# VectorE's order in an attention loop: transposes of projection inputs moved behind the next maxima, two small operations moved to GpSimd, statistics and residual additions moved later

## The chip, the core and the metric

The kernel runs on one core of a Trainium2 chip. The metric is the device time of one execution in microseconds (us); comparisons use the median of several runs. The engines are TensorE (PE; PEld is its weight load), VectorE (DVE), ScalarE (ACT), GpSimd (POOL) and SyncE (SP, which here only issues DMAs).

## The reference

x and ctx have shape [4, 1024, 512], all in fp32.

```python
def reference(x, ctx, Wq, bq, Wk, bk, Wv, bv, Wo, bo, clip_x, clip_down, w_gate, w_up, w_down):
    x = x + xattn(layernorm(x), ctx, ...)       # 16 heads of 32
    x = x + ffn(layernorm(x), ...)              # inner width 1408
    return x
# xattn: q = xn@Wq+bq; k, v = ctx@Wk+bk, ctx@Wv+bv; softmax(q k^T / sqrt(32), masked) @ v; @Wo+bo
# mask: rows 0..767 ("image") attend within their own block of 256; rows 768..1023 ("text")
#       attend to all image columns and causally to text columns
# ffn:  quant(x) = clip(round(x/s), -128, 127)*s, s = sigmoid(clip)*max|x|/127, over the whole tensor
#       weights quantised likewise by row; h = quant(silu(xq@Wg.T) * (xq@Wu.T)); h @ Wd.T
```

## The kernel before, in words

**Units and steps.** The attention is cut into 112 units. A unit is one of the four groups of four heads, for one block of 256 query rows of one batch element; a text block has four parts per group, an image block one. So a batch has 12 image units and 16 text units, and the last batch takes one image block, then text, then two image blocks. The loop `for n in range(len(units) + V_LAG)` makes one step per unit. In step n it issues, in this order:

1. `maxima(units[n])`: the scores s on PE (L449 for image, L460 for text) into PSUM, and their negated row maxima nmh on DVE (L453; L471 with the mask's addition L470). After a unit's last part, `minus_maxima` splits the maxima into two bf16 terms (L481 for text, a cast L488, a subtraction L489), and `shifts` transposes them to nmt (L496) and sends four small DMAs from SP to nmT (L501).
2. One item of the `background` deque: the layer norm of a chunk of 256 rows of x in three items (statistics on DVE L368 and L369, `deviation` on ACT and POOL L373 to L382, `apply` on ACT with the write to xn_d), or a weight's scale (L689 to L691 on DVE) and quantisation (POOL L695).
3. `large(n)`: one part of a projection on PE (pp_q, pp_kv, pv, and po for outputs, all at L229 in a helper). The bank that they write is freed by ACT's copies, or by the addition xr on DVE (L636).
4. Weights of unit n-5: the scores again, transposed (t), with the shift put in by a matmul of nmT (L534) and the products (L539), then exp on ACT (L544, L549); POOL sums the results into sp (L523).
5. Values of unit n-6 (av, L583 and L602), whose quotient (reciprocal L617 on DVE, product oT L618 on POOL) follows in the next step.
6. At the end of the step, `small_step`: a DVE transpose (L270) turns a loaded, spread projection input into qT or kvT, which the next projection reads. It runs only if `can_small(n)`: its load must have been sent in an earlier step. Then `prepare_next(n)` sends the load of the following one (L147, a single buffer), and a `weight_unit` may be queued.

From step 84 (`LATE`) on, projections are made in halves. After the loop come the second layer norm's scales, the FFN (pg and pu at L1219, silu L1227, h L1262, its maximum L1264) and the down stage (pd L1371).

**Who sets the order.** PE, DVE, ACT and POOL run in the order in which the program issues their instructions (`manual_schedule`), so an instruction that waits holds all that follow it on its engine. SP's DMAs are ordered by the scheduler. Scores and transposed scores share three PSUM buffers: t of unit n-5 can go on only when the maxima of unit n have been read.

**The down stage.** For each block of 512 tokens four tiles are multiplied. For each tile DVE quantises a group of the next block's h (L1345, with ACT's cast L1346), scales the product (sd, L1379) and adds it to the residual (L1380). After the block, POOL's queue gets the reload of a spilled h block (L1388) and then the block's output (L1390).

Of the kernel before, what the change touches and what calls it, by code (L numbers as in the profile page):

```python
# [14 lines left out]
ALU = mybir.AluOpType  # L15
# [9 lines left out]
NIC = FF // P  # L25
# [17 lines left out]
def kernel(ctx: ExitStack, tc: tile.TileContext, x, kv, Wq, bq, Wk, bk, Wv, bv, Wo, bo, clip_x, clip_down, w_gate, w_up, w_down, out):  # L43
    nc = tc.nc
# [78 lines left out]
    with ExitStack() as actx:  # L123
# [230 lines left out]

        background = deque()
        ready = {}

        def normalise(c):

            st = small.tile([P, 2, 6], F32, tag="st", name=f"st_{c}")  # L360
            mv = small.tile([P, 2, 2], F32, tag="mv", name=f"mv_{c}")
            s = small.tile([P, 2], F32, tag="ln_s", name=f"ln_s_{c}")
            t = small.tile([P, 2], F32, tag="ln_t", name=f"ln_t_{c}")
            xb = xbs[c]

            def statistics():
                for i in range(2):
                    nc.vector.bn_stats(st[:, i, :], xb[:, i, :])  # L368
                    nc.vector.bn_aggr(mv[:, i, :], st[:, i, :])  # L369

            def deviation():

                nc.scalar.activation(s, mv[:, :, 1], AF.Ln, bias=eps)  # L373
                nc.scalar.activation(s, s, AF.Exp, scale=-0.5)
                v = mv[:, :, 1]
                nc.gpsimd.tensor_scalar_add(v, v, EPS)
                nc.gpsimd.tensor_tensor(t, s, s, ALU.mult)
                nc.gpsimd.tensor_tensor(t, t, v, ALU.mult)
                nc.gpsimd.tensor_scalar(t, t, -0.5, 1.5, ALU.mult, ALU.add)
                nc.gpsimd.tensor_tensor(s, s, t, ALU.mult)  # L380
                nc.gpsimd.tensor_tensor(t, s, mv[:, :, 0], ALU.mult)
                nc.gpsimd.tensor_scalar_mul(t, t, -1.0)  # L382

            def apply():
                for i in range(2):
                    nc.scalar.activation(xb[:, i, :], xb[:, i, :], AF.Identity, bias=t[:, i : i + 1], scale=s[:, i : i + 1])
                if c > 0:
                    nc.sync.dma_start(xn_d[c].rearrange("(t p) c -> p t c", p=P), xb)
                ready[c] = True

            background.extend((statistics, deviation, apply))

        normalise(0)

# [80 lines left out]
        def minus_maxima(u):  # L475

            k, g = u.k, u.g
            nmh = state.pop((k.n, g)).rearrange("p h j i s -> p (h j) i s")
            if k.text:
                nm = small.tile([P, 4, 2], F32, tag="nm", name=f"nm_{u.n}")  # L480
                nc.vector.tensor_reduce(nm, nmh, AX.X, ALU.min)  # L481
            else:
                nm = nmh[:, :, :, 0]
            nm = nm.rearrange("p j i -> p i j")
            nm2 = nm2s[turn[0] % NMB]
            turn[0] += 1
            terms = nm2[:, :, :8].rearrange("p i (j d) -> p i j d", d=2)
            nc.vector.tensor_copy(terms[:, :, :, 0], nm)  # L488
            nc.vector.tensor_tensor(terms[:, :, :, 1], nm, terms[:, :, :, 0], ALU.subtract)  # L489
            u.nm2 = nm2  # L490

        def shifts(u):

            k, g, nm2 = u.k, u.g, u.nm2
            nmt = nmp.tile([P, 2, D], BF16, tag="nmt", name=f"nmt_{u.n}")
            nc.vector.transpose(nmt.rearrange("p i q -> p (i q)"), nm2.rearrange("p i r -> p (i r)"))  # L496
            nmT = nmTs[turnT[0] % len(nmTs)]
            turnT[0] += 1
            rows = nmT[0:P:16, :].rearrange("r (i q) -> r i q", i=2)
            for a in range(4):  # L500
                nc.sync.dma_start(rows[:, :, a * D : (a + 1) * D], nmt[a * D : a * D + 8])  # L501
            state["T", k.n, g] = nmT
# [244 lines left out]
        def can_small(n):  # L747
            return at_small < len(jobs) and at_small <= at_big + 1 and prepared.get(at_small, n) < n
# [164 lines left out]
        for n in range(len(units) + V_LAG):  # L913
            if n < len(units):
                u = units[n]
                half = u.part % 2
                for c in u.k.keys[2 * half : 2 * half + 2] if u.k.text else u.k.keys:
                    need_rows("k", c, u.g, n)
                need_rows("q", u.k.c, u.g, n)
                maxima(u)  # L920
                if u.part == u.parts - 1:
                    minus_maxima(u)
                    shifts(u)
            if n in (2, 3, 4, 5):
                (spread, sigmoids, product, total)[n - 2]()

            for first in (True, False):
                starts = [5 if first else 7] + [(7 if first else 9) + 4 * c for c in range(1, B * NQB)]
                if n not in starts:
                    continue  # L930
                c = starts.index(n)
                rows = slice(c * QB, (c + 1) * QB)
                if first:
                    nc.sync.dma_start(x1_d[rows, :].rearrange("(t p) c -> p t c", p=P), bo_b.unsqueeze(1).to_broadcast([P, QB // P, C]))
                else:
                    nc.gpsimd.dma_start(x1_d[rows, :], x_tok[rows, :], accum_op=ALU.add, max_dma_last_dim=C)
            t = units[n - T_LAG] if T_LAG <= n < LATE else None
            crowded = t is not None and t.k.text and t.part > 1
            f = background.popleft() if background and n > 0 and not (crowded and background[0].__name__ == "deviation") else None
            if f is not None and f.__name__ in ("deviation", "apply", "quantise"):  # L940
                f()
                f = background.popleft() if background and f.__name__ == "quantise" else None
# [50 lines left out]
                tail_products(0, (-1, 0, 1))  # L993
                tail_products(1, (-1, 0, 1))

            if can_small(n):
                small_step()
            prepare_next(n)
            if n > 8 and n_weights < 2 * NIC and quantised[0] and len(weight_stages) < 4 and len(background) < 2:
                stages = weight_unit(n_weights)  # L1000
                background.extend(stages)
                n_weights += 1
            if n < LATE and spent + BIG < target(n) and can_big(n + 1):
                early[0] = n < T_LAG
# [344 lines left out]
        quantise_h(order[0], i0, i1)  # L1349
    nc.vector.tensor_mul(scale_h, sig["h"], amax_h)  # L1350
    nc.vector.tensor_scalar_mul(srow, srow, scale_h)
    for n, tb in enumerate(order):
        hq, xr = steps(resident[tb]), xrs.pop(tb)
        after = order[n + 1] if n + 1 < NTB else None
        pos = [ps_d.tile([P, C], F32, tag="po", name=f"pd_{tb}_{t}") for t in range(NTT)]
        if n == 0:
            for ic in range(NIC):
                for t in range(NTT):
                    nc.tensor.matmul(pos[t], hq[:, ic, t * P : (t + 1) * P], wdT[:, ic, :], start=(ic == 0), stop=(ic == NIC - 1))
            for g in GROUPS:  # L1360
                quantise_h(after, *g)
        o = out_tok[tb * TB : (tb + 1) * TB, :].rearrange("(t p) c -> p t c", p=P)
        for t in range(NTT):
            parts = [(pos[t], slice(0, C))]
            if after is None and t == NTT - 1:
                more = ps_d.tile([P, C], F32, tag="po", name="pd_more")
                parts = [(pos[t], slice(0, C // 2)), (more, slice(C // 2, C))]
            if n:
                for po, cols in parts:
                    for ic in range(NIC):  # L1370
                        nc.tensor.matmul(po[:, cols], hq[:, ic, t * P : (t + 1) * P], wdT[:, ic, cols], start=(ic == 0), stop=(ic == NIC - 1))  # L1371

            if n > 1 and after is not None and t < len(GROUPS):
                quantise_h(after, *GROUPS[t])
            elif n == 1 and t < len(GROUPS) - 1:
                quantise_h(after, *GROUPS[t + 1])
            s = f3.tile([P, C], F32, tag="silu", name=f"sd_{tb}_{t}")
            for po, cols in parts:
                nc.vector.tensor_tensor(s[:, cols], po[:, cols], srow[:, cols], ALU.mult)  # L1379
                nc.vector.tensor_tensor(xr[:, t, cols], xr[:, t, cols], s[:, cols], ALU.add)  # L1380
                if after is None:
                    nc.sync.dma_start(o[:, t, cols], xr[:, t, cols])
            if n == 0 and t == 1:
                quantise_h(order[2], *GROUPS[0])
        if n < len(h_d):
            again = order[RESIDENT + n]
            resident[again] = hp.tile([P, NIC, TB], F32, tag="h", name=f"h2_{again}")
            nc.gpsimd.dma_start(resident[again], h_d[again])  # L1388
        if after is not None:
            nc.gpsimd.dma_start(o, xr)  # L1390
        if n + 4 < NTB:
            xrs[order[n + 4]] = load_x1(fr, order[n + 4])

# [39 lines left out]
```

## Time and profile before

| | |
|---|---|
| median of 3 runs | 1150.16 us (1150.04 to 1150.48) |
| profiled execution | 1149.1 us, its span 1147.4 us |
| mean granted TensorE clock | 0.997 |
| busy: PE, DVE, ACT, POOL | 1121.3, 878.4, 518.6, 513.2 us |
| steps 8, 12, 84 begin at | 92.11, 134.56, 683.32 us |

Busy times come from one profiled execution. Step times are the start of the step's first score matmul in the trace.

### The profile page before, as it was taken

How to read it: one execution, taken by the hardware profiler on the slowest of the kernel's cores; microseconds unless marked ns; L12 is line 12 of the kernel's file. 1: busy time of each engine (PE TensorE's matmuls, PEld its weight loads, DVE VectorE, ACT ScalarE, POOL GpSimd, SP SyncE). 2: the span in 40 equal slices, each digit the busy share in tenths (PEclk: the TensorE clock that was granted, in tenths of full speed). 3: DMA queues.
4: the chain of work that ended last, by engine and by line, in shares of the span. 5: the costliest groups of instructions: out<-in, count | busy, mean ns of one | idle time of the engine just before them, and what ended most of it. 6: DMA issues, size and time to landing. Idle time of an engine off the chain costs nothing.

```text
span 1147.4 us, 32558 instructions
## 1 busy us (share of the span) xinstructions
PE 1121.3 (98%) x14039; PEld 567.2 (49%) x14039; DVE 878.4 (77%) x1218; ACT 518.6 (45%) x731; POOL 513.2 (45%) x545
## 2 busy tenths in 40 slices
PE   9998999999999999999999999999999999999998
PEld 5544545454545545454544445555545444444444
DVE  2655777778887868798777767878976788887887
ACT  3333434244544434444433345544433566574553
POOL 1122446577654467775445576557642222020010
PEclk9999999999999999999999999999999999999999
DMA  7259334343434332453332113112211466200895
GB/s 230 94 191 283 92 94 112 75 112 94 94 61 109 94 94 62 111 106 75 94 80 75 40 61 85 42 40 87 84 67 56 175 232 225 87 26 1 309 387 192
DMA packets 111864, 132.67 MB, mean 116 GB/s; under 512 B 24156, under 2 KB 76392, under 8 KB 110312
## 3 DMA queue, kind: packets, MB, share of 16 engines
q1 hardware_dynamic: 89344, 89.16, 24.9%
q0 software_dynamic: 22064, 40.90, 13.3%
q8 instruction: 110, 1.80, 0.7%
q10 hardware_dynamic: 312, 0.53, 0.2%
q14 instruction: 34, 0.28, 0.1%
HBM read 84.29 MB, written 54.39 MB: 121 GB/s over the span
## 4 chain that ended last, share of the span: by engine, by line
PE 79%; DVE 11%; DMA 4%; issue 2%; POOL 1%; ACT 1%; SPq 1%; DVEq 0%; ACTq 0%; POOLq 0%
PE pv L229 9%; PE pp_kv L229 8%; PE pp_q L229 8%; PE av L583 8%; PE po L229 7%; PE t L539 7%; PE pg L1219 6%; PE pu L1219 6%; PE s L460 5%; PE s L449 3%; PE t L534 3%; PE av L602 3%; PE pd L1371 2%; DVE nmh L453 2%; DMA xt<-x_d 2%
## 5 line engine op out<-in xcount | busy, mean ns | idle before, releaser
L544 ACT ACTIVATE pT<-t 128x1024 f32<-128x1024 f32 x112 | 114.8, 1025 | 336.6 <-PE t L539 307.0
L523 POOL TENSOR_TENSOR sp<-sp,pT 128x1024 f32<-128x1024 f32 (+1 forms) x104 | 192.0, 1847 | 48.9 <-ACT pT L549 44.7
L471 DVE TENSOR_REDUCE nmh<-s 128x2 f32<-128x1024 f32 (+1 forms) x128 | 145.0, 1154 | 52.4 <-PE s L460 50.2
L523 POOL TENSOR_TENSOR sp<-pT 128x1024 f32<-128x1024 f32 x59 | 140.4, 2379 | 96.0 <-ACT pT L549 65.3
L453 DVE TENSOR_REDUCE nmh<-s 128x4 f32<-128x1024 f32 x96 | 112.3, 1212 | 46.2 <-PE s L449 46.2
L229 PE MATMUL pp_q<-qT,Wq_sb 128*32 128x256 f32 x2048 | 121.3, 380 | 0.2
L229 PE MATMUL pv<-Wv_sb,kvT 128*32 128x512 f32 (+1 forms) x1088 | 120.5, 570 | 0.0
L583 PE MATMUL av<-pT,va 128*32 128x256 f32 (+1 forms) x1792 | 117.7, 380 | 0.0
L229 PE MATMUL pp_kv<-kvT,Wk_sb 128*32 128x256 f32 x1920 | 112.6, 380 | 3.6 <-DVE xr L636 3.5
L539 PE MATMUL t<-qT,kT 32*128 32x256 f32 (+1 forms) x1792 | 116.0, 370 | 0.0
L618 POOL TENSOR_TENSOR oT<-avs 128x256 f32<-128x256 f32 x63 | 46.8, 742 | 153.4 <-DVE avs L617 153.4
L549 ACT ACTIVATE pT<-t 128x1024 f32<-128x1024 f32 x112 | 114.5, 1022 | 0.0
L229 PE MATMUL po<-Wo_sb,oT 128*32 128x512 f32 (+1 forms) x1120 | 112.1, 534 | 0.5 <-DVE xr L636 0.2
L617 DVE RECIPROCAL avs<-avs 128x256 f32<-128x256 f32 x63 | 108.8, 1727 | 0.0
L539 PEld LDWEIGHTS t<-qT,kT 32*128 32x128 f32 x1792 | 89.3, 185 | 5.8
L1219 PE MATMUL pg<-xqT,wgT 128*128 128x512 bf16 x344 | 88.1, 379 | 1.3 <-ACT silu L1227 1.3
L1219 PE MATMUL pu<-xqT,wuT 128*128 128x512 bf16 (+1 forms) x348 | 88.3, 376 | 0.5 <-DVE h L1262 0.4
L229 PEld LDWEIGHTS pp_q<-qT,Wq_sb 128*32 128x32 f32 x2048 | 63.3, 110 | 48.3 <-issue 5.8
L229 PEld LDWEIGHTS pp_kv<-kvT,Wk_sb 128*32 128x32 f32 x1920 | 59.7, 110 | 48.3 <-DVE xr L636 4.9
L1262 DVE SCALAR_TENSOR_TENSOR h<-pu,su,silu 128x512 f32<-128x512 f32 (+1 forms) x89 | 64.8, 736 | 21.6 <-PE pu L1219 14.7
L1227 ACT ACTIVATE silu<-pg,sg 128x512 f32<-128x512 f32 x88 | 60.4, 686 | 46.4 <-PE pg L1219 39.0
L583 PEld LDWEIGHTS av<-pT,va 128*32 128x32 f32 x1792 | 47.3, 109 | 53.5 <-issue 30.6
(214 smaller groups left out, 1566.0 us busy)
## 6 DMA issues: line engine op xcount, KB each, us to landing
xt<-x_d SPq DMA_DIRECT2D x16, 1024.0 KB
h<-h_d POOLq DMA_DIRECT2D x3, 2816.0 KB, 13.4
xb<-in_x_dram SPq DMA_DIRECT2D x16, 512.0 KB
x_d<-bo_b SPq DMA_DIRECT2D x16, 512.0 KB
x_d<-in_x_dram POOLq DMA_DIRECT2D x16, 512.0 KB, 6.9
xr<-x_d SPq DMA_DIRECT2D x16, 512.0 KB
spread_kv<-in_ctx_dram SPq DMA_DIRECT2D x60, 128.0 KB
xn_d<-xb SPq DMA_DIRECT2D x15, 512.0 KB
```

The lines of the kernel that those rows point to most:

```text
L229: nc.tensor.matmul(out[rows_of(j)], lhs[:, rows_of(j)], rhs, start=start, stop=stop, tile_position=(0, j * D), skip_group_check=True)
L453: nc.vector.tensor_reduce(nmh[:, h, :, :, 0], prs[h], AX.X, ALU.max, negate=True)
L471: nc.vector.tensor_reduce(nmh[:, h, :, i, half], s[:, :, :n], AX.X, ALU.max, negate=True)
L523: nc.gpsimd.tensor_tensor(sp[:, :, cols], a, pT[:, :, n, cols], ALU.add)
L539: nc.tensor.matmul(prs[j // 2][:, j % 2, n, cols], kc[rows_of(j), g, n * P : (n + 1) * P], q[rows_of(j), g, cols], start=False, stop=(n == 1))
L544: nc.scalar.activation(pT[:, :2], prs[0], AF.Exp)
L549: nc.scalar.activation(pT[:, 2:], prs[1], AF.Exp)
L583: nc.tensor.matmul(av[rows_of(j), 0, cols], va[:, n, g * P + j * D : g * P + (j + 1) * D], u.pT[:, j, n, cols], start=(u.part == 0 and n = ...
L617: nc.vector.reciprocal(avs[:, 1, :], avs[:, 1, :])
L1219: nc.tensor.matmul(ps, w[:, cc, ic * P : (ic + 1) * P], qT[:, cc, :], start=(cc == 0), stop=(cc == NCC - 1))
L1227: nc.scalar.activation(s, pg, AF.Silu, scale=sg[:, ic : ic + 1])
L1262: nc.vector.scalar_tensor_tensor(h[:, ic, cols], pu[:, cols], su[:, ic : ic + 1], s[:, cols], ALU.mult, ALU.mult)
```

## The change

- `normalise` notes the step in which a chunk's load was sent (`sent_in`); in the first 16 steps its statistics, renamed `chunk_statistics`, are not taken up until two steps later.
- In `minus_maxima`, the two term operations of image units go from DVE to POOL. For text units they stay on DVE, and the cast becomes a maximum of the value with itself.
- `shifts` of an image unit (a DVE transpose and four DMAs) moves into the next step, behind the next unit's maxima.
- `small_step` moves from the end of step n to behind the maxima and shifts of step n+1.
- A weight unit may be queued from step 6 (before: 9), and with up to two items waiting (before: one); in the late steps it goes to the front of the deque.
- In the down stage the residual addition of a tile follows the next tile's scaled product, and the block's output DMA is issued ahead of the reload of h on POOL's queue.

PE's instructions and their order stay as they were; DVE has 96 instructions less in the loop and POOL 96 more.

```diff
@@ normalise
+            sent_in[c] = unit[0]
-            def statistics():
+            def chunk_statistics():
@@ minus_maxima
-            nc.vector.tensor_copy(terms[:, :, :, 0], nm)
-            nc.vector.tensor_tensor(terms[:, :, :, 1], nm, terms[:, :, :, 0], ALU.subtract)
+            if k.text:
+                nc.vector.tensor_tensor(terms[:, :, :, 0], nm, nm, ALU.max)
+                nc.vector.tensor_tensor(terms[:, :, :, 1], nm, terms[:, :, :, 0], ALU.subtract)
+            else:
+                nc.gpsimd.tensor_copy(terms[:, :, :, 0], nm)
+                nc.gpsimd.tensor_tensor(terms[:, :, :, 1], nm, terms[:, :, :, 0], ALU.subtract)
@@ loop over steps
                 if u.part == u.parts - 1:
                     minus_maxima(u)
-                    shifts(u)
+                    if u.k.text:
+                        shifts(u)
+            previous = units[n - 1] if 0 < n <= len(units) else None
+            if previous is not None and not previous.k.text:
+                shifts(previous)
+            if n and can_small(n - 1):
+                small_step()
...
+            unit[0] = n
-            f = background.popleft() if background and n > 0 and not (crowded and background[0].__name__ == "deviation") else None
+            name = background[0].__name__ if background else None
+            young = name == "chunk_statistics" and n < 16 and n - max(sent_in.values()) < 2
+            f = background.popleft() if background and n > 0 and not young and not (crowded and name == "deviation") else None
...
-            if can_small(n):
-                small_step()
             prepare_next(n)
-            if n > 8 and n_weights < 2 * NIC and quantised[0] and len(weight_stages) < 4 and len(background) < 2:
+            if n > 5 and n_weights < 2 * NIC and quantised[0] and len(weight_stages) < 4 and len(background) < 3:
                 stages = weight_unit(n_weights)
-                background.extend(stages)
+                if n < LATE:
+                    background.extend(stages)
+                else:
+                    background.extendleft(reversed(stages))
@@ down stage
                 nc.vector.tensor_tensor(s[:, cols], po[:, cols], srow[:, cols], ALU.mult)
-                nc.vector.tensor_tensor(xr[:, t, cols], xr[:, t, cols], s[:, cols], ALU.add)
                 if after is None:
+                    nc.vector.tensor_tensor(xr[:, t, cols], xr[:, t, cols], s[:, cols], ALU.add)
                     nc.sync.dma_start(o[:, t, cols], xr[:, t, cols])
+            def residual(xr=xr, t=t, s=s, o=o):
+                nc.vector.tensor_tensor(xr[:, t, :], xr[:, t, :], s, ALU.add)
+                if t == NTT - 1:
+                    nc.gpsimd.dma_start(o, xr)
+            if left is not None:
+                left()
+            left = residual if after is not None else None
+            if left is not None and t == NTT - 1:
+                left()
+                left = None
...
-        if after is not None:
-            nc.gpsimd.dma_start(o, xr)
```

More of the change, by code (lines that the diff above doesn't have):

```diff
@@ L356 @@
         ready = {}
+        unit, sent_in = [0], {}
         def normalise(c):
@@ L389, in apply @@
                 ready[c] = True
-            background.extend((statistics, deviation, apply))
+            background.extend((chunk_statistics, deviation, apply))
         normalise(0)
@@ L1379 @@
                 nc.vector.tensor_tensor(s[:, cols], po[:, cols], srow[:, cols], ALU.mult)
-                nc.vector.tensor_tensor(xr[:, t, cols], xr[:, t, cols], s[:, cols], ALU.add)
                 if after is None:
+                    nc.vector.tensor_tensor(xr[:, t, cols], xr[:, t, cols], s[:, cols], ALU.add)
                     nc.sync.dma_start(o[:, t, cols], xr[:, t, cols])
+            def residual(xr=xr, t=t, s=s, o=o):
[7 more added lines that the diff above has]
+                left()
+                left = None
             if n == 0 and t == 1:
```

## The prediction

> **What bounds the kernel now.** I read the page first, then the waits of PE, then the waits of DVE, then the timeline around each wait. A step below is a round of the attention loop (step n computes the score maxima of unit n). The page's first part says who sets the end:
>
> ```profile
> PE 1121.3 (98%) x14039; PEld 567.2 (49%) x14039; DVE 878.4 (77%) x1218; ACT 518.6 (45%) x731; POOL 513.2 (45%) x545
> ```
>
> TensorE is busy for 1121.3 of 1147.4 us. A reordering of VectorE can only touch the 26 us in which PE is idle, or the clock. PE's waits (engine, line, waited-for line: total us, times, longest) show which part of that VectorE causes:
>
> ```profile
> PE t L534 <- DVE nmh L453: 7.3, 6, 4.4
> PE pp_kv L229 <- DVE xr L636: 3.5, 3, 1.4
> PE t L534 <- DVE nmh L471: 2.2, 2, 1.8
> ...
> PE pd L1371 <- ACT h L1346: 1.1, 2, 0.8
> ```
>
> The timeline places them. Of the first and third rows (9.5 together), 4.42 lie in step 8 (97.2 to 101.6), 0.51 in step 5, and the other 4.6 in steps 84 to 111; the largest of these is 1.81 in step 96. The second row is steps 19, 47 and 75 (1.03, 1.03, 1.43). The cause of the 4.42 stands in DVE's waits, and a transpose comes behind it:
>
> ```profile
> DVE st L368 <- DMA xb<-in_x_dram: 12.2, 3, 5.9
> ```
>
> DVE waits 5.95 for a chunk of x at its statistics, transposes qT (2.00), and only then reduces the maxima for which PE holds its score bank. This idle also costs clock (columns: us; PE, PEld, DVE, ACT and POOL busy; granted clock; DMA share; GB/s):
>
> ```profile
> 98.63:102.04 3.41, 0.46 (x10) 0.46 (x13) 3.41 (x3) 1.04 (x4) 1.42 (x7) 1.00 0.94 352
> 102.04:105.45 3.41, 3.41 (x36) 1.72 (x32) 2.84 (x5) 1.94 (x2) 0.38 (x1) 0.50 1.04 375
> ...
> 890.52:893.93 3.41, 1.62 (x8) 0.63 (x7) 2.70 (x10) 2.62 (x6) 1.28 (x6) 1.00 0.29 71
> 893.93:897.35 3.42, 3.27 (x8) 1.13 (x8) 2.70 (x7) 1.52 (x3) 0.80 (x1) 0.50 0.75 296
> ```
>
> After a stretch of 3.41 us with 0.46 us of PE work, the next one was granted half the clock: 36 matmuls where the next full one has 68, so 1.7 us lost. 1.62 us of work led to the same; the stretch before, with 1.95, did not.
>
> **The change, part by part** (against the profiled 1149.1; its span is 1147.4, and the median lies 1.06 above it).
>
> *Young rule, steps 5 and 8.* Statistics wait two steps after the load is sent, so the DMA waits of DVE go: step 5's 0.51 and step 8's 4.42 end. What is late next in step 8 is new: the changed order puts the transpose kvT into step 8, behind nmh and nmt, while PE's order is unchanged and goes from s straight to pp_kv, which reads that kvT. Before, kvT was made two steps ahead. The same holds in step 12, where before kvT was made at the end of step 10 and PE did not wait. In the changed order all other transposes lie a step or more before their use, or behind pv, t and av of the same step (steps 6 and 10).
>
> *Price of a kvT in its own step.* An undisturbed image step shows it:
>
> ```profile
> 128.45 2.36 DVE L453 TENSOR_REDUCE nmh<-s 128x4 f32<-128x1024 f32 x2 [2.87 <-PE s L449]
> 130.84 0.17 DVE L488 CAST nm<-nmh 128x8 bf16<-128x8 f32 x1
> 131.05 0.17 DVE L489 TENSOR_TENSOR nm<-nmh,nm 128x8 bf16<-128x8 f32 x1
> 131.26 0.24 DVE L496 STREAM_TRANSPOSE nmt<-nm 128x64 bf16<-128x64 bf16 x1
> ```
>
> Its s began at 127.27, the next matmul at 128.35, and nmh ended 3.54 after the start of s. Then come nmt (0.24) and kvT, 2.14 by its mean row, with about 0.04 between: kvT ends at +5.96, and PE has been free since +1.08. That is 4.9 idle. In step 8 it replaces 4.42: +0.5. In step 12 (text maxima of 2.33, the same) it is new: +4.9. Nothing covers it, since only s precedes it.
>
> *Clock.* By the rows an idle of 4.9 cannot be spread over two stretches so that both keep 1.62 us of work (that allows 3.6), so step 12 pays a half-speed stretch too: at most 1.7, and 1.25 if PE begins late within it; I take 1.5. Step 8 paid it already. The one at the tail (893.93) depends on where the grid falls: 0, and down to -1.7 in the range. In the Trainium skill, "TensorE: Matmul & The Clock Gate", section "What's actually happening", the half clock follows a whole idle window of about 3.4 us on a free-running grid; 4.9 us of idle then contains one in 1.5 of 3.4 placements, and step 12's term would be about 0.7, an estimate from that page. The rows above disagree with it, as no stretch there was wholly idle, and I keep the rows.
>
> *Small steps behind the next maxima.* qT at the end of steps 18, 46 and 74 held xr (L636), which frees the projection bank. Step 19: -1.0; step 47: after the change a qT lies between nmt and xr, +0.1; step 75: -0.2. Sum -1.1. In the late steps the transposes and terms no longer precede the maxima that PE waits for: of 4.6 I leave 0.6 (steps 107 to 111, where weight scales and statistics still queue), so -4.0; 5.4 is all PE idle between 683 and 850, the bound. New crowding: in steps 40 and 68 DVE would carry nmh 2.36, nmt 0.24, qT 2.1, a weight transpose 0.71, avs 1.73 and statistics with xm 2.1, in all 9.2 with gaps, in a step of 7.29. It starts the next maxima some 1.9 late. In step 9 (109.28) PE first needed them at +4.0 (113.3) and had them at +2.4 (111.69), so they may be some 1.6 late, and some 0.3 to 0.5 is left, twice; steps 29 and 57 (a qT and two statistics ahead of xr) about 0.3 each. +1.6, range 0 to 3.2.
>
> *Terms on GpSimd.* 48 units lose L488 (17.0) and L489 (17.5) from DVE: 34.5 us, none of it on the path but what is counted above. GpSimd gets 96 short operations; its nearest rows, 128x2, take 189 to 225 ns, so 0.45 per unit and 21 in all beside 513 busy. Behind them in its queue stand the next sp, oT and deviation. DVE reads the terms only after the next unit's maxima, some 7 us later, and the longest sp pair is 4.83: 0, up to 3.5 if the late steps (5.4 to 6.3 long) are too short. The four DMAs of nmT on SP go out one step later, still four steps ahead of t; 0.
>
> *Text: max instead of cast.* The cast waits for GpSimd:
>
> ```profile
> L488 DVE CAST nm<-nm 128x8 bf16<-128x8 f32 x16 | 19.7, 1233 | 0.5
> ...
> 288.35 4.83 POOL L523 TENSOR_TENSOR sp<-sp,pT 128x1024 f32<-128x1024 f32 x2 [1.73 <-ACT pT L549]
> ...
> 290.99 2.22 DVE L489 TENSOR_TENSOR nm<-nmh,nm 128x8 bf16<-128x8 f32 x1
> ```
>
> It takes 0.17 alone and 1.233 on average, ending with an sp. But the last row, a TENSOR_TENSOR with two operands, also lasted until that sp ended (293.18), so the max, with two operands too, should wait likewise: 0 saved. Were it free, 17 us would leave DVE, and at the places above 0.3 would reach PE.
>
> *Earlier weight units.* The same operations in other steps; counted under crowding.
>
> *Down stage.* The residual of a tile now follows the next quantise and product, and the output's DMA stands ahead of the h reload on POOL's queue. Before, PE waited 0.28 and 0.79 at pd (the 1.1 row). The quantise comes 0.69 (one add) earlier: -0.5. The reload goes out 3 to 6 us later but lands 6 or more before its use: range -1.1 to +1.
>
> **Sum**: -0.5 + 0.5 + 4.9 + 1.5 - 1.1 - 4.0 + 1.6 + 0 + 0 - 0.5 = +2.4, so 1151.5 in a profiled execution and 1152.6 as a median.
>
> **Rivals.** *Not slower: DVE has room after step 12.* It loses 34.5 us, and if that fills every crowded step (1.6 goes) and all late idle ends (5.4 instead of 4.0), the sum is -0.6: 1149.6; with the tail's half-speed stretch gone by the grid, 1147.9, and with the down stage at its best, 1147.3. For it: idle of DVE in the image steps (2.87 ahead of nmh above). Against: 20.61 busy of 23.71 between 683 and 707.
>
> *Slower: GpSimd's terms come too late.* In the 12 image steps of the last batch the terms stand behind an sp pair of 4.83 in steps of 5.4 to 6.3; DVE stands at nmt in order, with kvT, scales and avs behind it. The longest wait of a DVE operation behind one sp is 2.2, PE tolerates 1.6 to 1.9, so up to 0.6 each; at half of 7, +3.5: 1156.1. It decides once the terms end later than the next maxima. Against: between 753 and 818 POOL is busy for 40.35 of 64.98.
>
> *The changed operations don't unload the late steps*: the text terms wait as before and half of the 4.6 stays: +1.7, 1154.3.
>
> **How the numbers follow.** About 0.2% (2.3 us) is what a measurement of this kernel can tell from no change. Forecast 0.40 (0.17 of it within that bound, 0.23 slower; own range 1150.5 to 1155); not slower 0.34 (0.22 faster, 0.12 same); late terms 0.17 (slower); late steps not unloaded 0.09 (0.02 same, 0.07 slower). Faster 0.22, same 0.31, slower 0.47. The low end is the first rival with the step-12 stretch at its cheapest and xr's waits gone, 1146.5; the high end is the second with crowding and down stage at their worst, 1158.5.
>
> **What would show it.** Right: PE's waits list pp_kv behind kvT (L270) twice with 4.5 to 5 each, a half-speed stretch after each, no DMA wait at the statistics of steps 5 to 8, and less than 1.5 left of t behind nmh. The text terms keep a mean near 1.2. Wrong: no wait on kvT (then about 1146), waits of DVE at nmt for GpSimd, or new waits at pp_kv behind xr of over 3 in sum.

## The result, and the profile after

The changed kernel takes 1156.82 us (median of 4 runs, 1155.19 to 1157.5) against 1150.1 of the kernel before: a ratio of 1.0054, 95% interval 1.0041 to 1.0067. It is slower by 6.7 us. The forecast was 1152.6, slower by 2.5, with a range that reached 1158.5. The direction and most of the mechanism held; the size was 4 us short.

The waits of PE in the changed kernel (its line numbers are a few higher: xr is now L642, t L540, nmh L455 and L473):

```profile
PE pp_kv L229 <- DVE kvT L270: 9.1, 2, 4.6
PE pp_kv L229 <- DVE xr L642: 8.0, 4, 3.0
...
PE po L229 <- DVE xr L642: 0.9, 1, 0.9
PE t L540 <- DVE nmh L473: 0.9, 2, 0.7
...
PE t L540 <- DVE nmh L455: 0.5, 1, 0.5
```

The waits of t behind nmh, 9.5 before, are down to 1.4: 4.9 of that were the waits of steps 5 and 8, which the later statistics end even without the moved transposes (`e1` below), and the rest lay in the late steps. Two waits on kvT, which the kernel before did not have, cost 9.1, and the waits of pp_kv for xr have risen from 3.5 to 8.0.

The second wait on kvT, in step 12, on DVE and then on PE:

```profile
134.88 2.36 DVE L473 TENSOR_REDUCE nmh<-s 128x2 f32<-128x1024 f32 x2 [3.15 <-PE s L462]
137.15 0.23 DVE L502 STREAM_TRANSPOSE nmt<-nm 128x64 bf16<-128x64 bf16 x1
137.31 1.95 DVE L270 STREAM_TRANSPOSE kvT<-spread_kv 128x1024 f32<-128x1024 f32 x1
```

```profile
133.70 1.15 PE L462 MATMUL s<-kT,qT 32*128 32x256 f32 x16
139.41 1.94 PE L229 MATMUL pp_kv<-kvT,Wk_sb 128*32 128x256 f32 x16 [4.56 <-DVE kvT L270]
```

PE has nothing between the scores and a projection that reads what DVE makes third. The clock around these waits, in steps 8 and 12, in stretches of 3.41 us laid where the granted clock changes (busy times of PE, PEld, DVE, ACT, POOL, then the granted clock):

```profile
93.59:97.00 3.41, 0.00 (x0) 0.00 (x0) 3.41 (x5) 1.25 (x2) 2.13 (x3) 1.00 1.16 171
97.00:100.41 3.41, 3.22 (x32) 1.79 (x36) 1.68 (x2) 0.00 (x0) 0.74 (x1) 0.50 0.85 265
...
134.55:137.96 3.41, 0.30 (x8) 0.00 (x0) 3.08 (x4) 2.50 (x4) 2.35 (x1) 1.00 0.00 0
137.96:141.37 3.41, 1.96 (x20) 1.15 (x24) 3.41 (x3) 0.00 (x0) 0.00 (x0) 0.50 0.46 163
141.37:144.79 3.42, 3.42 (x36) 1.83 (x32) 0.12 (x1) 0.00 (x0) 0.73 (x1) 0.50 0.57 153
```

One half-speed stretch follows the idle of step 8 and two follow that of step 12. After a half-speed stretch with 3.22 us of PE work full speed came back; after the one with 1.96, into which the end of the idle reached, it did not.

Where the 7.6 us between the two spans lie, from the starts of the steps' first score matmuls in the two traces (us; "forecast" adds the prediction's terms for that stretch; the work ahead of step 0 took 0.2 less after the change):

| stretch | before | after | change | forecast |
|---|---|---|---|---|
| steps 0 to 12 | 110.74 | 117.35 | +6.6 | +6.4 |
| steps 13 to 83 | 541.47 | 547.83 | +6.4 | +0.5 |
| steps 84 to 110 | 159.01 | 153.93 | -5.1 | -4.0 |
| step 111 to the end | 305.06 | 304.94 | -0.1 | -0.5 |

The second row is the miss. Within it, step 47 lost 3.4, step 75 lost 1.6, step 15 lost 1.0, steps 29 and 57 lost 1.1 together, steps 24 and 52 gained 0.8, and step 19, where 1.0 was forecast to go, did not move. Step 47 on DVE, and the sp additions of POOL beside it, before:

```profile
400.83 2.20 DVE L270 STREAM_TRANSPOSE qT<-spread_q 128x1024 f32<-128x1024 f32 x1 [1.80 <-PE pp_q L229]
...
406.45 1.07 DVE L488 CAST nm<-nm 128x8 bf16<-128x8 f32 x1
407.56 0.17 DVE L489 TENSOR_TENSOR nm<-nm,nm 128x8 bf16<-128x8 f32 x1
407.76 0.24 DVE L496 STREAM_TRANSPOSE nmt<-nm 128x64 bf16<-128x64 bf16 x1
407.93 0.65 DVE L636 TENSOR_TENSOR xr<-po,xr 128x512 f32<-128x512 f32 x1
```

```profile
402.67 4.82 POOL L523 TENSOR_TENSOR sp<-sp,pT 128x1024 f32<-128x1024 f32 x2 [2.27 <-ACT pT L549]
```

and after, with POOL beside it:

```profile
413.09 2.16 DVE L491 TENSOR_TENSOR nm<-nm 128x8 bf16<-128x8 f32 x1
415.28 0.17 DVE L492 TENSOR_TENSOR nm<-nm,nm 128x8 bf16<-128x8 f32 x1
415.49 0.24 DVE L502 STREAM_TRANSPOSE nmt<-nm 128x64 bf16<-128x64 bf16 x1
415.67 2.02 DVE L270 STREAM_TRANSPOSE qT<-spread_q 128x1024 f32<-128x1024 f32 x1
417.60 0.66 DVE L642 TENSOR_TENSOR xr<-po,xr 128x512 f32<-128x512 f32 x1
```

```profile
410.41 4.81 POOL L529 TENSOR_TENSOR sp<-sp,pT 128x1024 f32<-128x1024 f32 x2 [2.87 <-ACT pT L555]
```

The text term's first operation ends only when the second of POOL's two sp additions has ended: at 407.52, where that one ended at 407.49, and after the change at 415.25 against 415.22. The transpose that stood ahead of the maxima before was therefore free: it only used up time that DVE would otherwise have stood in the term. After the change DVE comes to the term earlier and stands in it for 2.16 instead of 1.07, and the transpose now comes behind it, ahead of xr. PE waits 3.0 for xr instead of 1.0, and a half-speed stretch (from 417.85 to 421.27) adds the rest of the 3.4.

### The profile page after: what moved, and what is told of

Read it like the earlier page. It is cut to its first block, busy times and chain, and to the rows that moved or that the text cites. A ratio compares the mean times of both kernels' runs of the same rounds, so it can differ in the third digit from the quotient of the medians.

```text
span 1155.0 us, 32521 instructions
## 1 busy us (share of the span) xinstructions
PE 1119.9 (97%) x14016; PEld 568.7 (49%) x14039; DVE 839.3 (73%) x1122; ACT 517.3 (45%) x731; POOL 531.8 (46%) x641
## 4 chain that ended last, share of the span: by engine, by line
PE 83%; DVE 7%; DMA 3%; issue 3%; POOL 2%; ACT 2%; ACTq 0%; SPq 0%; DVEq 0%; POOLq 0%
PE pp_kv L229 10%; PE pp_q L229 10%; PE pv L229 9%; PE av L589 8%; PE t L545 7%; PE po L229 7%; PE pg L1236 6%; PE pu L1236 6%; PE s L462 5%; PE s L451 4%; PE t L540 3%; PE av L608 3%; PE pd L1389 2%; DMA xt<-x_d 2%; POOL sp L529 1%
## 5 line engine op out<-in xcount | busy, mean ns | idle before, releaser
L473 DVE TENSOR_REDUCE nmh<-s 128x2 f32<-128x1024 f32 (+1 forms) x128 | 145.2, 1156 | 65.8 <-PE s L462 63.6
L455 DVE TENSOR_REDUCE nmh<-s 128x4 f32<-128x1024 f32 x96 | 112.9, 1218 | 100.1 <-PE s L451 100.1
L229 PE MATMUL pp_kv<-kvT,Wk_sb 128*32 128x256 f32 x1920 | 118.2, 394 | 17.2 <-DVE kvT L270 9.1
L545 PE MATMUL t<-qT,kT 32*128 32x256 f32 (+1 forms) x1792 | 113.2, 367 | 0.0
L229 PEld LDWEIGHTS pp_kv<-kvT,Wk_sb 128*32 128x32 f32 x1920 | 62.1, 114 | 65.2 <-issue 18.2
```

The lines of the kernel that those rows point to most:

```text
L229: nc.tensor.matmul(out[rows_of(j)], lhs[:, rows_of(j)], rhs, start=start, stop=stop, tile_position=(0, j * D), skip_group_check=True)
L455: nc.vector.tensor_reduce(nmh[:, h, :, :, 0], prs[h], AX.X, ALU.max, negate=True)
L473: nc.vector.tensor_reduce(nmh[:, h, :, i, half], s[:, :, :n], AX.X, ALU.max, negate=True)
L545: nc.tensor.matmul(prs[j // 2][:, j % 2, n, cols], kc[rows_of(j), g, n * P : (n + 1) * P], q[rows_of(j), g, cols], start=False, stop=(n == 1))
```

## The experiments

The theory: the loss lies in the place of the transposes, ahead of their own pp_kv in steps 8 and 12, and ahead of xr in text steps, where the term's wait for GpSimd sets the time. Rivals: the idle only moves to another wait, or the other parts of the change carry the loss.

**Transposes back at the end of the step** (`e1`).

```diff
-            if n and can_small(n - 1):
-                small_step()
...
+            if can_small(n):
+                small_step()
             prepare_next(n)
```

> The changed kernel with small_step back at the end of step n, all else as changed. Theory (the new waits come from the place of the transposes): the two waits of pp_kv on kvT go with their half-speed stretches (about 6.6 in step 8 and 7.3 in step 12), the waits for xr in steps 47 and 75 fall from 3.0 to about 1.0 to 1.4 (4 to 5 with the clock), the late waits behind nmh come back for 3.5 to 5: 1141 to 1145 us. Rival (the other parts of the change cost the time): still above 1150 us.

Measured: 1147.58 us, ratio to the kernel before 0.998 (0.9971 to 0.9989). Against the changed kernel step 8 gains 6.2, step 12 gains 7.3, step 47 gains 3.4 and step 75 gains 1.6, near what was expected, and steps 84 to 110 take 159.21, as before the change. But step 10 loses 3.3 to a wait of 2.9 behind nmh that neither kernel had, so the sum is some 3 us short. The loss belongs to the move, in steps 8 and 12 together with the later statistics (`e8` below).

**Early at the start only** (`e2`): at the end of the step up to step 12, behind the maxima from 13 on.

```diff
-            if n and can_small(n - 1):
+            if n >= 13 and can_small(n - 1):
                 small_step()
...
+            if n < 13 and can_small(n):
+                small_step()
```

> The changed kernel with small_step at the end of the step up to step 12 only, and behind the maxima from step 13 on. Theory (steps 8 and 12 alone carry the loss of the start): no wait on kvT, no half-speed stretch in steps 8 to 13, 13 to 14 us less than the changed kernel: 1143 to 1144 us, below the kernel before. The waits for xr in steps 19, 47 and 75 stay at 1.1, 3.0 and 3.0. Rival (the idle moves to the next wait behind DVE, as the load wait of step 8 did): a gain of at most 7 us, 1150 us.

Measured: 1149.73 us, 0.9995 (0.9981 to 1.0008). The two waits on kvT are gone (steps 8 and 12: 6.2 and 7.3), and step 10 gives 6.5 back. Both views were half right: the load wait is not gone, it now stands at a transpose:

```profile
115.06 1.99 DVE L270 STREAM_TRANSPOSE qT<-spread_q 128x1024 f32<-128x1024 f32 x1 [6.03 <-DMA spread_q<-xn_d]
116.98 2.31 DVE L455 TENSOR_REDUCE nmh<-s 128x4 f32<-128x1024 f32 x2
```

With statistics two steps later the normalised rows are written and read back later too, so a qT at the end of step 9 waits 6.03 for its load, ahead of the next maxima.

**Text terms on GpSimd, shifts one step later** (`e3`).

```diff
-            if k.text:
-                nc.vector.tensor_tensor(terms[:, :, :, 0], nm, nm, ALU.max)
-                nc.vector.tensor_tensor(terms[:, :, :, 1], nm, terms[:, :, :, 0], ALU.subtract)
-            else:
-                nc.gpsimd. ...
+            nc.gpsimd.tensor_copy(terms[:, :, :, 0], nm)
+            nc.gpsimd.tensor_tensor(terms[:, :, :, 1], nm, terms[:, :, :, 0], ALU.subtract)
...
-            if previous is not None and not previous.k.text:
+            if previous is not None and previous.part == previous.parts - 1:
                 shifts(previous)
```

> The changed kernel with the terms of text units on GpSimd too and their shifts in the next step. Theory (the text maximum of DVE is held until an sp addition of GpSimd ends, and holds xr behind it): xr no longer waits for it; the wait of pp_kv for xr goes in step 19 (1.1) and falls from 3.0 to about 0.9 in steps 47 and 75, where the transpose stays ahead of xr; with the half-speed stretch of step 47 gone 6 us less, 1151 us. Rival (the transpose alone holds xr): the three waits change by less than 0.5 each, 1156 us.

Measured: 1152.49 us, 1.0026 (1.0016 to 1.0036). Steps 19, 47 and 75 gain 1.3, 4.0 and 2.5, together 7.7, more than expected. The waits of PE:

```profile
PE pp_kv L229 <- DVE kvT L270: 9.1, 2, 4.6
PE t L536 <- DMA nmT<-nmt: 2.8, 4, 1.7
PE t L536 <- DVE nmh L455: 2.1, 2, 1.6
PE pp_kv L229 <- DVE xr L638: 2.0, 3, 0.9
```

xr's wait falls from 8.0 to 2.0, with the transpose still ahead of xr, so the transpose alone did not hold it. In the short late steps nmT now lands too late for t (2.8), and steps 84 to 110 lose 4.3 of what the change had gained there.

**Both** (`e4`).

> The changed kernel with small_step early up to step 12 and the text terms on GpSimd. Theory: both gains add up, 19 to 20 us less than the changed kernel, 1137 us, about 13 less than the kernel before. Rival: text terms behind sp come too late for the shifts in the short late steps, so the late waits of DVE at nmt eat 3 us or more: 1140 us or more.

Measured: 1144.04 us, 0.9947 (0.993 to 0.9964). The gains add, less the 6.7 of step 10, which `e2` had shown, and 2.9 in steps 84 to 110, where t waits 2.6 for the DMA of nmT: 7 us above the expectation. The rival is right that the text terms come too late there, but what waits is t, and DVE's waits list none at nmt.

**kvT early, qT behind the maxima, up to step 12** (`e5`).

```diff
-            if n and can_small(n - 1):
+            if n and can_small(n - 1) and (n >= 13 or jobs[at_small].kind == "q"):
                 small_step()
...
+            if n < 13 and can_small(n) and jobs[at_small].kind == "kv":
+                small_step()
```

> The changed kernel, but in steps 0 to 12 a kvT is made at the end of a step and a qT behind the maxima. Theory (a kvT must not lie ahead of its own pp_kv, a qT must not lie ahead of the load of its normalised rows): neither the two waits on kvT nor the wait of qT for its load in step 9 that the kernel with all transposes early showed: 13 to 14 us less than the changed kernel, 1143 us, 6 less than with all transposes early. Rival (one of the loads is late wherever its transpose stands): a wait of 3 us or more at t or pp_kv remains in steps 6 to 13, 1147 us or more.

Measured: 1147.02 us, 0.9976 (0.9962 to 0.9991), ten runs from 1142.63 to 1149.71. Step 10 loses 1.6 instead of 6.5: its qT waits 2.9 for its load and pp_q 1.4 for it. Steps 8 and 12 gain their 13.4. The profiled run paid half-speed stretches at 407 and 622, in steps 47 and 75; of these two the changed kernel's paid only the first. Two of the ten runs met 1143 (1142.63 and 1143.34); the median misses it by 4. The 1147 that the rival gave fits the time, but not by the wait that it named, which is 1.4.

**The same, with text terms on GpSimd up to step 83** (`e6`, and again `e11`).

```diff
-        def minus_maxima(u):
+        def minus_maxima(u, fast=False):
...
-            if k.text:
+            if fast:
                 nc.vector.tensor_tensor(terms[:, :, :, 0], nm, nm, ALU.max)
...
-                    minus_maxima(u)
-                    if u.k.text:
+                    fast = u.k.text and n >= LATE
+                    minus_maxima(u, fast)
+                    if fast:
                         shifts(u)
-            if previous is not None and not previous.k.text:
+            if previous is not None and previous.part == previous.parts - 1 and not (previous.k.text and n > LATE):
                 shifts(previous)
```

> The same with the terms of text units on GpSimd and their shifts in the next step up to step 83, and as changed from step 84 on, where the steps are short and t soon wants nmT. Theory: the waits for xr in steps 19, 47 and 75 fall by 1.1, 2.1 and 2.1 and the half-speed stretch of step 47 goes, and the waits of t for the DMA of nmT (2.6 where all text terms were on GpSimd) do not come: 1136 to 1138 us. Rival: the late waits behind nmh stay without them, 1139 us or more.

> The kernel with kvT early and text terms on GpSimd up to step 83 a second time, beside the one with the transposes behind xr, since its four times lay 5.6 us apart: a median of 1138 to 1141 us, 0.8 to 1.0% less than the kernel before. If the first profile's time was the rule and not the exception, 1136 us.

Measured: 1140.52 us (1135.62 to 1141.24), 0.9909 (0.9885 to 0.9933), and the second time 1138.5 us (1137.52 to 1139.8), 0.9899 (0.9883 to 0.9916): about 1% faster than the kernel before. The waits of PE, the second time:

```profile
PE pp_q L229 <- DVE qT L270: 2.4, 1, 2.4
PE pp_kv L229 <- DVE xr L642: 2.0, 3, 0.9
PE t L540 <- DVE nmh L455: 1.9, 2, 1.5
```

What is left is qT's load in step 10 (2.4 here, none of note in the first profile), 2.0 at xr and 1.9 at t behind nmh, 1.5 of it in step 87. The waits for xr fell as expected and the late DMA wait is gone (0.2 or less). The first median still lies 2.5 above the expected 1136 to 1138, where the rival had it, and the second 0.5 above it.

**Transposes behind xr** (`e9`), from step 13 on, in the last kernel.

```diff
-            if n and can_small(n - 1) and (n >= 13 or jobs[at_small].kind == "q"):
+            if n and n < 13 and can_small(n - 1) and jobs[at_small].kind == "q":
                 small_step()
...
             for g in fs:
                 g()
+            if n >= 13 and can_small(n - 1):
+                small_step()
```

> As the kernel with kvT early and text terms on GpSimd up to step 83, but from step 13 on the transposes stand behind xr of the same step, not ahead of it. Theory (what is left of the waits for xr is the transpose ahead of it): the three waits of pp_kv for xr of 0.9 in steps 47, 75 and 87 go, 2 us less than that kernel: 1138 to 1139 us where it gives 1140.5. Rival: the transposes then stand ahead of the next maxima again, and the late waits behind nmh come back, 2 us or more slower than that kernel.

Measured: 1142.66 us, 0.9936 (0.9922 to 0.9951), where the kernel beside it gave 1138.5. The rival holds: xr's waits go, and t waits 5.7 behind the text maxima (L473) in seven places; step 96 alone loses 2.8. None of the three places tried from step 13 on (behind the maxima, behind xr, at the end of the step) costs nothing.

**Image terms back on DVE** (`e7`), all else as changed.

```diff
-                nc.gpsimd.tensor_copy(terms[:, :, :, 0], nm)
-                nc.gpsimd.tensor_tensor(terms[:, :, :, 1], nm, terms[:, :, :, 0], ALU.subtract)
+                nc.vector.tensor_copy(terms[:, :, :, 0], nm)
+                nc.vector.tensor_tensor(terms[:, :, :, 1], nm, terms[:, :, :, 0], ALU.subtract)
```

> The changed kernel with the terms of image units back on DVE, shifts and small_step as changed. Theory (the late waits went because the transposes no longer stand ahead of the maxima, and the 34 us off DVE are worth nothing by themselves): within 1.5 us of the changed kernel, 1155.5 to 1158.5 us. Rival (the room on DVE is what ended the late waits): 3 to 5 us more, 1160 us or more.

Measured: 1160.93 us, 1.0095 (1.0079 to 1.0112), 4.1 above the changed kernel. My theory fell: the terms' place is worth what the rival said. Steps 84 to 110 take 158.8 instead of 153.9. In step 96 the transposes' move keeps its gain; in steps 101 to 109 the terms wait for POOL and hold xr and the next maxima:

```profile
834.89 2.22 DVE L495 TENSOR_TENSOR nm<-nmh,nm 128x8 bf16<-128x8 f32 x1
837.02 0.23 DVE L502 STREAM_TRANSPOSE nmt<-nm 128x64 bf16<-128x64 bf16 x1
837.18 0.38 DVE L642 TENSOR_TENSOR xr<-po,xr 128x256 f32<-128x256 f32 x1
```

```profile
832.22 4.85 POOL L529 TENSOR_TENSOR sp<-sp,pT 128x1024 f32<-128x1024 f32 x2
```

With the first experiment (terms on GpSimd, transposes at the end, 159.21) this shows that neither part alone brings the late gain of 5; both are needed.

**Statistics as before** (`e8`): no waiting of two steps.

```diff
-            young = name == "chunk_statistics" and n < 16 and n - max(sent_in.values()) < 2
+            young = False and name == "chunk_statistics" and n < 16 and n - max(sent_in.values()) < 2
```

> The changed kernel without the rule that statistics wait two steps. The order then has the kvT in steps 7 and 11, one step ahead of their use. Theory (the rule delays the chunk, the chunk its qT, and that the kvT behind it): no waits on kvT and no half-speed stretches in steps 8 and 12, 12 to 14 us less than the changed kernel: 1143 to 1145 us; DVE waits for xb again, but behind the maxima, where it costs PE under 1 us. Rival (the load wait that the rule removes comes back into PE's path): 4 us or more of idle in steps 5 to 9, 1149 us or more.

Measured: 1146.69 us, 0.9971 (0.9959 to 0.9984). Steps 0 to 12 gain 13.4 with no wait on kvT: the rule, with the moved transposes, is what put kvT into the step of its use. DVE waits 5.3 for xb in sum, and PE's list names none of it. The price is elsewhere: a qT now stands between nmt and xr in step 19 too (from 188.63 for 2.01), where PE now waits 3.0 instead of 1.1; with a half-speed stretch (from 191.69) that costs 3.6. Steps 47 and 75 lose 1.5 and 1.7 more with the same waits of 3.0, to half-speed stretches (two from 406.73, one from 625.18). So the time stays 2 us above the theory's.

**Text cast instead of the maximum** (`e10`).

```diff
-                nc.vector.tensor_tensor(terms[:, :, :, 0], nm, nm, ALU.max)
+                nc.vector.tensor_copy(terms[:, :, :, 0], nm)
```

> The changed kernel with the cast of text terms instead of the maximum of the value with itself. Theory (both wait until the sp addition of GpSimd that runs when they start has ended): the cast's mean duration is 1.3 to 1.5 us as the maximum's 1.39, and the time is within 1.5 us of the changed kernel's 1156.8. Rival (the maximum, with two operands from the memory, waits more than the cast): xr waits shorter in steps 19, 47 and 75, 2 us or more less.

Measured: 1156.73 us, 1.0058 (1.0043 to 1.0073), against 1156.82 with the maximum. The two operations, the cast first and the maximum of the changed kernel second:

```profile
L491 DVE CAST nm<-nm 128x8 bf16<-128x8 f32 x16 | 22.3, 1391 | 0.5
```

```profile
L491 DVE TENSOR_TENSOR nm<-nm 128x8 bf16<-128x8 f32 x16 | 22.3, 1391 | 0.5
```

The means agree to a nanosecond: for these two operations what they wait for sets the length, not which of them it is.

## Why the prediction was right, and where it was short

**kvT in its own step: right.** 4.9 idle in steps 8 and 12 was forecast; PE's waits show 9.1 in sum, 4.6 each, a little less because kvT took 1.95 instead of 2.14 and began before nmt had ended. Step 8 came out at -0.25 instead of +0.5, step 12 at +7.3 instead of +6.4: there two half-speed stretches followed, some 2.7 us lost by the work in them (half of 1.96 + 3.42), where I took 1.5 us of one. The working had shown that at least one must follow, and stopped there; it did not ask whether the work left in that one is enough to bring full speed back.

**The clock rule.** The Trainium skill, "TensorE: Matmul & The Clock Gate", section "What's actually happening", puts the half clock behind an idle window of about 3.4 us. One window here was wholly idle (93.59 to 97.00), but those with 0.30 and 0.85 us of work (134.55 to 137.96, 414.44 to 417.85) were each followed by half the clock too. The measurement decides, as it did in the prediction.

**xr in steps 19, 47 and 75: the step that failed.** I put -1.1, and the changed kernel shows +5.0 (0, +3.4, +1.6). The working took the transpose at the end of the step before as what held xr. What held it was the text term, whose end POOL's sp sets; I had that wait in hand (the cast's 1.233 mean) and priced it as cost per operation, not as a time before which DVE can't pass. With a fixed end, work ahead of it is free, and work moved behind it counts in full. Two runs show it: text terms on GpSimd take 7.7 us off these three steps with the transposes where they are, and transposes at the end of the step take off the 5.0 with the terms where they are. In step 47 PE waits 3.0 for xr with both ahead of it, 1.0 with the term alone (`e1`), 0.5 with the transpose alone (`e3`) and not at all with neither (`e9`). The prediction had named new waits behind xr of over 3 in sum as a sign of being wrong, and they rose by 4.5.

**New crowding: near in size, by luck.** +1.6 was forecast for steps 29, 41, 57 and 69. Steps 29 and 57 lost 1.1, more than the 0.6 put there; steps 41 and 69 lost nothing that shows, and step 15, which the working did not name, lost 1.0.

**The late steps: right.** -4.0 forecast, -5.1 measured. The working counted the transposes and the terms together there, as no longer ahead of the maxima, and neither alone does it: with the terms back on DVE 4.9 of the 5.1 go (158.8 against 153.93), and with the transposes back all of it (159.21).

**The text maximum: right.** 0 saved was forecast, and 1156.73 against 1156.82 shows it. The mean of the first operation, expected to stay near 1.2, rose to 1.39; in step 47 DVE comes to it earlier.

**GpSimd's terms too late: did not happen.** They take 199 and 209 ns, as the rows of 189 to 225 had it, and no wait of DVE at nmt for GpSimd stands among DVE's waits.

**Down stage.** From the first pd matmul to the end 80.9 instead of 81.6: -0.8 against -0.5. The stretch before it, from step 111, gave back most of that (224.1 instead of 223.4). No run takes out this part, or the earlier weight units, by itself.

**The size: not by the working.** 1156.8 lies above the forecast's own 1150.5 to 1155. Its high end of 1158.5 left room above that for late terms on GpSimd, worse crowding and a poor down stage, and none of them came; what filled the room was xr and the second half-speed stretch, so that the number lies below that end is luck. The two ends don't follow from the terms named with them either: these give about 1159.2 and 1144.7, not 1158.5 and 1146.5. The direction holds without that: steps 0 to 12 lost 6.6 and the late steps gained 5.1.

## What to carry to other kernels

An in-order engine that meets an instruction which ends at a time set by another engine has a fixed point there: work ahead of it is free as long as it fits before that end, work behind it costs in full, so look for such ends before moving anything past them. When a producer is moved later for the sake of one wait, list for each of its results the first instruction that reads it and what stands between; a rule that delays the head of a chain (statistics, write, load, transpose) moves every link, and two harmless moves can add to one that isn't. A stall of 3 to 5 us on TensorE cost its length here, and none, one or two half-speed stretches behind it.

## What the runs showed of the hardware that I had not expected

A 4.6 us idle of TensorE was followed by 3.4 us of half clock in step 8 (from 97.00) and by 6.8 us in step 12 (from 137.96) of one execution, with the same idle in both. A 3.0 us idle (step 47, the first two rows) drew 3.4 us of it, and one of the same length in step 75 (the last two) none:

```profile
414.44:417.85 3.41, 0.85 (x16) 0.26 (x8) 3.34 (x5) 1.89 (x2) 2.16 (x2) 1.00 0.01 1
417.85:421.27 3.42, 2.95 (x28) 1.38 (x32) 0.41 (x1) 0.00 (x0) 3.33 (x2) 0.50 0.40 114
...
629.48:632.89 3.41, 1.87 (x35) 0.85 (x28) 3.34 (x4) 1.94 (x2) 2.16 (x2) 1.00 0.00 0
632.89:636.30 3.41, 1.93 (x36) 1.20 (x40) 2.34 (x5) 0.00 (x0) 3.33 (x2) 1.00 0.19 50
```

The idle of step 75 fell on the border of two stretches, and each kept more work. With stretches laid like this in all thirteen profiles, once full speed has begun, each full-speed stretch with up to 1.66 us of PE work was followed by half speed, and each with 1.76 or more was not (both in `e1`, at 754.75 to 758.17 and 113.05 to 116.46). A half-speed stretch with 2.81 was followed by another (`e2`, from 117.61), one with 2.87 by full speed (`e2`, from 411.16). So the same stall costs more or less by where it falls, and the kernels with such stalls spread: ten times of `e5`, which has the waits of 3.0 in steps 47 and 75, lay between 1142.63 (mean granted clock 0.999) and 1149.71 (0.994).
